# Layer 2's window attention: two windows on the partitions for values and exponentials, their outputs from one 128-row product, the softmax sums beside them

## The chip, the cores and the metric

The kernel runs on one core of one Trainium2 chip, in fp32 throughout. The metric is the device time of one launch in microseconds, the median of several runs. Numbers from "the profile" come from one profiled execution of the kernel, which has a time of its own. The engines are named as in the profile: PE (matrix products; PEld are its weight loads), DVE, ACT, POOL, and SP, which issues most DMAs.

## The reference

Four layers follow one another on 4 images of 192 channels and 64 x 64 pixels: a deformable convolution with channel attention and an MLP (layer 0), a non-local attention (layer 1), an attention over overlapping windows with a gated MLP (layer 2) and a masked, input-dependent 3 x 3 convolution (layer 3). The change is in the window attention of layer 2. Cut to that:

```python
y = _conv1x1(_ln_c(x, n1g, n1b), qkv_w, qkv_b)          # 3*192 channels a pixel
cols = _unfold(y, WS, STRIDE, PAD)                      # windows of 8x8, 6 apart, 3 padding: 11 x 11 of them
win = cols.reshape(B, 3 * HEADS, ch, WS * WS, L).transpose(0, 4, 1, 3, 2)
attn = jnp.einsum('blhic,blhjc->blhij', q, k) + bias    # 6 heads of 32 channels, 64 x 64 pixels
e = jnp.exp(attn - jnp.max(attn, axis=-1, keepdims=True))
s_img = _reverse(jnp.sum(e, axis=-1, keepdims=True), H, W)   # sums, added up over overlapping windows
o = jnp.einsum('blhij,blhjc->blhic', e, v)
o_img = _reverse(o, H, W).reshape(B, HEADS, ch, H, W)        # outputs, added up likewise
out = (o_img / s_img[:, :, None]).reshape(B, C, H, W)
```

## The kernel before, in words

Each image goes through the layers in turn. Layer 0 of the next image is woven into layer 1 of this one and into the end of this one; the window attention, `windows(b, ...)` (L1050), runs alone, between layer 1 and the projection behind it. Inside it the program order is kept by hand (`tc.manual_schedule()`, L1282): every engine takes its instructions in the order in which the loop at L1305 writes them, and only the buffers of a pool are handed out by a planner, which goes by its own costs.

The loop goes over 11 strip rows of windows (`wr`), and in a row over three groups `g` of four windows (the last group has three; a fourth is computed twice and its second copy not used). What a row does, with the lines by which the profile knows it:

- `scores(wr, g)` (L1147): for each of four windows and six heads (3 `e` times 2 `h`) one product of 32 channels, query by key (L1157), into a PSUM tile of three banks, one for each `e`. Before, a window pair lies on the two halves of the partitions (query pixel i of one window on 0 to 63, of the other on 64 to 127), and `h` and key pixel j along the columns. Then DVE adds the position bias (L1164), takes the maximum (L1170) and subtracts it (L1171).
- `exponentials` (L1174): ACT's exponential (L1176), and DVE's two sums of each head (`es`, L1180). They are written one group ahead of use.
- `turned(wr, g, pair)` (L1186): for each of the two window pairs of a group the values: a product of the layer's input with the value weights (L1196), eight of them, so that the two head halves lie on the partitions and the windows side by side in the columns; ACT copies them out (`vs`, L1201). Then three 128 x 128 transposes of the exponentials (L1204) and ACT's copy of them (`et`, L1206). The last pair of a row has a single window.
- `outputs` (L1209), one pair later: for each window, `e` and `h` a product of 64 rows by 32 columns (L1221), which adds the window at its place into the strip `o` in PSUM, and for a pair one product of the sums with shifted identities `pixels` (L1228), which adds the sums into partitions 96 to 101 of the same strip.
- Between them: `norm` of a later row's new pixels (L394 mean, L398 difference, L401 square, L373 variance, L353 and L354 inverse root, L382 its spreading, L413 product), `project_rows` of the next row (L1121 and L1122, copied out by L1125 and L1127), `collect` (L1238, L1239, POOL's L1244), `inverses` (L1260, reciprocal L1264) and `finish` of the row before (L1270, DVE's L1273).

PSUM is fully taken: three banks for scores, two for the strip, one tagged "n" for the norm's products and `inverses`, and two tagged "a", which the values, the transposes, `project_rows` and `finish` share.

## Time and profile before

| | us |
|---|---|
| median of 9 runs | 6755.78 |
| lowest and highest of them | 6728.27 and 6790.15 |
| the profiled execution's own time | 6780.3 |
| its span, first to last instruction | 6778.5 |
| granted PE clock over the span | 0.949 |
| first window stage, 1637.5 to 1903.0 | 265.5, of which PE busy 250.41, DVE 159.86, ACT 119.85, POOL 69.01 |
| the four window stages together | 1074 |

Busy time is the union of an engine's instructions; a run of products is entered with its duration including the time in PE's pipeline, so it overlaps with the next. A span from the start of one block to the start of the next is the better measure of what a block takes, and the prediction uses such spans. In the timeline, "[0.83 <-DVE rs L1264]" after an instruction says that its engine sat idle for 0.83 us before it, and what ended that.

### The profile page before, as it was taken

Reading aid. Unit: us, or ns where it says so; the run is one execution under the profiler, and the core shown is the slowest. Engines: PE = TensorE matmul, PEld = TensorE weight load, DVE = VectorE, ACT = ScalarE, POOL = GpSimd, SP = SyncE. Lnnn points to the kernel's source line nnn. Section 1 sums busy time; section 2 is a strip of 40 time slices with the busy share of each in tenths; the row PEclk is TensorE's granted clock in tenths of the full one; section 3 lists DMA queues with packets and bytes.
Section 4 is the critical chain, followed back from the end, with each engine's and each line's share of the span. In section 5 each row is a group of like instructions: output and inputs, shape, how many; then the busy total and the mean of one; then the engine's idle time right before and its main releaser. Section 6 shows DMA issues by size and latency. Waiting matters only on the chain. (4 is left out here: it accounts for less than half of the span.)

```text
span 6778.5 us, 115795 instructions
## 1 busy us (share of the span) xinstructions
PE 6169.7 (91%) x45392; PEld 4192.4 (62%) x45392; DVE 4696.3 (69%) x6908; ACT 3604.1 (53%) x6136; POOL 2078.0 (31%) x2276
## 2 busy tenths in 40 slices
PE   7687999999989899999998899999998989999986
PEld 4445577877644467787654457878664457776532
DVE  3664258985586849896577848888567767765656
ACT  3664357874445348785445337777444435544332
POOL 2654047761200027773210007675220000002200
PEclk7788989999989999999999999999999999999998
DMA  6786156662010156663110046665100010001000
GB/s 181 254 275 192 46 158 214 212 207 59 10 43 15 42 176 198 220 204 114 33 30 22 19 121 220 210 212 170 38 22 27 17 58 10 15 18 31 4 7 21
DMA packets 330496, 699.37 MB, mean 103 GB/s; under 512 B 60077, under 2 KB 217181, under 8 KB 329182
## 3 DMA queue, kind: packets, MB, share of 16 engines
q0 software_dynamic: 92736, 455.22, 20.6%
q1 hardware_dynamic: 236382, 235.95, 12.2%
q8 instruction: 358, 5.87, 0.4%
q14 instruction: 188, 1.54, 0.1%
q10 hardware_dynamic: 832, 0.79, 0.0%
HBM read 611.25 MB, written 78.87 MB: 102 GB/s over the span
## 5 line engine op out<-in xcount | busy, mean ns | idle before, releaser
L616 POOL DMA_INDIRECT ring<-table,idx x1152 | 1649.2, 1432 | 1139.4 <-DVE row L623 241.9
L963 PE MATMUL s<-ths,ph 96*128 96x256 f32 x4096 | 993.0, 384 | 6.2 <-ACT ths L957 2.4
L963 PEld LDWEIGHTS s<-ths,ph 96*128 96x128 f32 x4096 | 786.2, 193 | 134.4 <-ACT ths L957 5.1
L622 ACT ACTIVATE row<-ring,pos 128x384 f32<-128x384 f32 x1152 | 673.6, 610 | 199.0 <-DVE xo L627 104.1
L1031 PE MATMUL y<-sc,gx 128*97 128x256 f32 x3008 | 728.0, 384 | 32.2 <-ACT yn L1037 27.0
L623 DVE SCALAR_TENSOR_TENSOR row<-ring,fr,row 128x384 f32<-128x384 f32 x1152 | 676.5, 615 | 89.6 <-ACT row L622 60.1
L1031 PEld LDWEIGHTS y<-sc,gx 128*97 128x97 f32 x3008 | 493.6, 166 | 166.7 <-ACT yn L1037 29.4
L626 ACT ACTIVATE xo<-row,pos 128x192 f32<-128x192 f32 x1152 | 488.2, 450 | 163.8 <-remote 71.3
L627 DVE SCALAR_TENSOR_TENSOR xo<-row,fr,xo 128x192 f32<-128x192 f32 x1152 | 449.0, 414 | 125.1 <-ACT xo L626 81.0
L1028 DVE TENSOR_TENSOR sc<-sc,mbs 128x1024 f32<-128x1024 f32 x376 | 454.1, 1220 | 45.1 <-issue 23.4
L965 ACT COPY sc<-s 128x1024 f32<-128x1024 f32 x376 | 377.7, 1005 | 170.8 <-PE s L963 146.2
L970 DVE TENSOR_TENSOR top<-top,sc 128x1024 f32<-128x1024 f32 x282 | 344.9, 1223 | 134.9 <-ACT sc L965 113.9
L634 PE MATMUL h<-ti,xo 128*128 128x192 f32 x2304 | 436.0, 328 | 0.0
L1029 ACT ACTIVATE sc<-sc 128x1024 f32<-128x1024 f32 x376 | 393.9, 1054 | 74.2 <-DVE sc L1028 65.9
L634 PEld LDWEIGHTS h<-ti,xo 128*128 128x128 f32 x2304 | 390.1, 190 | 29.0 <-issue 8.2
L1180 DVE TENSOR_REDUCE es<-ex 128x6 f32<-128x384 f32 x264 | 133.3, 546 | 363.4 <-ACT ex L1176 363.4
L634 PE MATMUL h<-kept,xo 128*128 128x192 f32 x960 | 251.7, 399 | 121.9 <-DVE xo L627 80.6
L634 PEld LDWEIGHTS h<-kept,xo 128*128 128x128 f32 x960 | 182.7, 223 | 212.2 <-DVE xo L627 110.3
L1624 POOL COPY gate<-gate 128x192 f32<-128x192 f32 x12 | 4.2, 351 | 1002.3 <-ACT gate L1617 1002.3
L1377 DVE SCALAR_TENSOR_TENSOR ga<-gate,v,ga 128x1024 f32<-128x1024 f32 x234 | 300.4, 1284 | 6.7
L858 ACT ACTIVATE gl<-h,bias_fc 128x256 f32<-128x256 f32 x384 | 151.2, 474 | 234.0 <-PE h L851 233.5
L1031 PE MATMUL y<-se,gx 128*97 128x256 f32 x1088 | 267.6, 387 | 6.6 <-ACT se L1029 6.0
(391 smaller groups left out, 11239.8 us busy)
## 6 DMA issues: line engine op xcount, KB each, us to landing
ti<-table SPq DMA_DIRECT2D x768, 48.0 KB
ring<-table,idx POOLq DMA_INDIRECT x1152
xnd<-xn SPq DMA_DIRECT2D x4, 3270.0 KB
xi<-in_x_dram SPq DMA_DIRECT2D x32, 384.0 KB
xk<-xd SPq DMA_DIRECT2D x32, 384.0 KB
xd<-xc SPq DMA_DIRECT2D x64, 192.0 KB
table<-tt SPq DMA_DIRECT2D x32, 384.0 KB
xc<-xd SPq DMA_DIRECT2D x60, 192.0 KB
```

What stands on the lines that cost most here:

```text
L616: nc.gpsimd.indirect_dma_start(out=gt.rearrange("p q r c -> p (q r c)"), out_offset=None, in_=corners, in_offset=bass.IndirectOffsetOnAxis ...
L622: nc.scalar.activation(row, gt[:, 0], AF.Copy, scale=pos[:, t, 9 + tap : 10 + tap])
L623: nc.vector.scalar_tensor_tensor(row, gt[:, 1], fr[:, t, 9 + tap : 10 + tap], row, ALU.mult, ALU.add)
L626: nc.scalar.activation(xo[:, j, :], row[:, 0, :], AF.Copy, scale=pos[:, t, tap : tap + 1])
L627: nc.vector.scalar_tensor_tensor(xo[:, j, :], row[:, 1, :], fr[:, t, tap : tap + 1], xo[:, j, :], ALU.mult, ALU.add)
L634: nc.tensor.matmul(acc[m // 2][:, bass.ts(m % 2, C)], lhsT=xo.rearrange("p j c -> p (j c)")[:, bass.ts(m, 128)], rhs=tt, start=t == 0 and ...
L963: nc.tensor.matmul(p[:, t, :], lhsT=ph[:, bass.ts(G * g + t, 128)], rhs=ths[i], start=True, stop=True)
L965: nc.scalar.copy(to, p)
L970: nc.vector.tensor_tensor(tops[i], tops[i], to, ALU.max)
L1028: nc.vector.tensor_tensor(ex, ex, mbs[i].unsqueeze(1).to_broadcast([128, G, QN]), ALU.add)
L1029: nc.scalar.activation(ex, ex, AF.Exp)
L1031: nc.tensor.matmul(py, lhsT=gx[:, G * g + t, :], rhs=ex[:, t, :], start=g == 0 and t == 0, stop=g == NG - 1 and t == G - 1,)
```

## The change

On the partitions of the scores now lie the two head halves `h`, with the windows along the columns. So the transposes yield two windows' key pixels on the 128 partitions, for the three `e` and two `h` in the columns. The values of both windows then come from one product per input half (128 columns of the array, 192 in the moving operand), and the outputs of both windows from one product of 128 rows for each `e` and `h`: the transposed exponentials `et` are written into a tile that is zero elsewhere, the second window six pixels to the right, so that one product of 8 x 14 pixels adds both windows. There are three such tiles an image, cleared once by POOL, and two ACT copies fill one, 64 partitions each. The sums are taken with one DVE instruction a group, spread over the two halves by a product with `side` (1 or 0), and added into the strip by one product for each window, written among the outputs. The bias is loaded directly in the new layout, and the products that keep PE busy at the stage's start (`keep_warm`) read another constant of the same size.

```diff
     for j in range(4):
...
-    pixels = const([128, WS, WS + STRIDE], "pixels")
-    nc.gpsimd.memset(pixels, 0.0)
-    for w in range(2):
-        to = pixels[:, :, STRIDE * w : STRIDE * w + WS]
-        nc.gpsimd.tensor_add(to, to, ident[:, bass.ts(w, WS * WS)].rearrange("p (r c) -> p r c", c=WS))
+    pixels = const([128, WS, WS], "pixels")
+    nc.gpsimd.tensor_add(
+        pixels.rearrange("p r c -> p (r c)"), ident[:, bass.ts(0, WS * WS)], ident[:, bass.ts(1, WS * WS)]
+    )
+    side = const([128, 2], "side")
+    nc.gpsimd.memset(side, 0.0)
+    for h in range(2):
+        nc.gpsimd.memset(side[64 * h : 64 * h + 64, h : h + 1], 1.0)
     eps = const([128, 1], "eps")
...
     headmask = const([P, P], "headmask")
...
-        bias = const([128, 3, 2, WS * WS], "bias")
+        bias = const([128, 3, WS * WS], "bias")
         N1 = 2 * WS - 1
...
             for e in range(HEADS):
...
                     rows = shifted[:, e, :].rearrange("p (r c) -> p r c", c=N1)[:, WS - 1 - ix : 2 * WS - 1 - ix, 0:WS]
-                    in_turn(nc.sync.dma_start(out=bias[WS * ix : WS * ix + WS, e % 3, e // 3, :], in_=rows))
+                    at = 64 * (e // 3) + WS * ix
+                    in_turn(nc.sync.dma_start(out=bias[at : at + WS, e % 3, :], in_=rows))
                 yield
-        in_turn(nc.sync.dma_start(out=bias[64:128], in_=bias[0:64]))
...
     def keep_warm(p, n):
         m, width = p.shape
-        columns = bias.rearrange("p e h j -> p (e h j)")[:, 0:width]
+        columns = spread.rearrange("p j n -> p (j n)")[:, 0:width]
         for _ in range(n):
...
                 sets.append((xs, qs, ks))
+            ets = []
+            for j in range(3):
+                et = s1.tile([128, 3, 2, WS, WS + STRIDE], F32, tag=f"et{j}", name=f"et{j}_{b}")
+                nc.gpsimd.memset(et, 0.0)
+                ets.append(et)
...
             nc.gpsimd.memset(headspread, 0.0)
...
                     for h in range(2):
...
                             rows = slice(32 * e, 32 * e + 32)
-                            at = 128 * (w // 2) + 64 * h
                             nc.tensor.matmul(
-                                p[64 * (w % 2) : 64 * (w % 2) + 64, e, at : at + 64],
+                                p[64 * h : 64 * h + 64, e, 64 * w : 64 * w + 64],
                                 lhsT=qw[rows, h, of, :], rhs=ks[rows, h, :, STRIDE * of : STRIDE * of + WS],
...
                 ex = sb.tile([128, 3, WG, 64], F32, tag="ex", name=f"ex_{b}_{wr}_{g}")
-                half = bias.rearrange("p e h j -> p e (h j)").unsqueeze(2).to_broadcast([128, 3, WG // 2, 128])
                 nc.vector.tensor_tensor(
-                    ex.rearrange("p e (v h) j -> p e v (h j)", h=2),
-                    p[:, :, 0:256].rearrange("p e (v n) -> p e v n", n=128), half, ALU.add,
+                    ex, p[:, :, 0 : 64 * WG].rearrange("p e (w j) -> p e w j", j=64),
+                    bias.unsqueeze(2).to_broadcast([128, 3, WG, 64]), ALU.add,
                 )
...
                 mx = sb.tile([128, 3 * WG], F32, tag="mx", name=f"mx_{b}_{wr}_{g}")
...
             def exponentials(wr, g, ex):
                 nc.scalar.activation(ex, ex, AF.Exp)
-                ex = ex.rearrange("p (e u) j -> p e u j", e=3)
-                sums = sb.tile([128, WG // 2, HEADS], F32, tag="sums", name=f"es_{b}_{wr}_{g}")
-                for pair in range(WG // 2):
-                    nc.vector.tensor_reduce(
-                        sums[:, pair, :].rearrange("p (e h) -> p e h", h=2), ex[:, :, 2 * pair : 2 * pair + 2, :],
-                        AX.X, ALU.add,
-                    )
-                return ex.rearrange("p e u j -> p e (u j)"), sums
+                half = sb.tile([128, WG, 3], F32, tag="half", name=f"eh_{b}_{wr}_{g}")
+                nc.vector.tensor_reduce(
+                    half.rearrange("p w e -> p e w"), ex.rearrange("p (e w) j -> p e w j", e=3), AX.X, ALU.add
+                )
+                sums = sb.tile([128, WG, HEADS], F32, tag="sums", name=f"es_{b}_{wr}_{g}")
+                nc.vector.tensor_tensor(
+                    sums.rearrange("p w (e h) -> p (w e) h", h=2),
+                    half.rearrange("p w e -> p (w e)").unsqueeze(2).to_broadcast([128, 3 * WG, 2]),
+                    side.unsqueeze(1).to_broadcast([128, 3 * WG, 2]), ALU.mult,
+                )
+                return ex.rearrange("p (e w) j -> p e (w j)", e=3), sums
...
                 wins = [w for w in (WG * g + 2 * pair, WG * g + 2 * pair + 1) if w < NWIN]
...
-                pv = ps2.tile([128, 512], F32, tag="a", name=f"v_{b}_{wr}_{g}_{pair}")
-                for i, w in enumerate(wins):
-                    for k in range(2):
-                        for h in range(2):
-                            nc.tensor.matmul(
-                                pv[64 * h : 64 * h + 64, bass.ts(i, P)], lhsT=xw[: P + k, k, w, :],
-                                rhs=qkvT[: P + k, k, 2 * C + P * h : 2 * C + P * h + P], start=k == 0, stop=k == 1,
-                            )
-                v = sb.tile([128, 2, P], F32, tag="v", name=f"vs_{b}_{wr}_{g}_{pair}", bufs=3)
-                nc.scalar.copy(v[:, 0:m, :], pv[:, 0 : m * P].rearrange("p (m c) -> p m c", m=m))
+                rows, both = slice(0, 64 * m), slice(wins[0], wins[0] + m)
+                pv = ps2.tile([128, 512], F32, tag="a", name=f"v_{b}_{wr}_{g}_{pair}")[rows, 0:C]
+                for k in range(2):
+                    nc.tensor.matmul(
+                        pv, lhsT=xw[: P + k, k, both, :].rearrange("p w j -> p (w j)"), rhs=qkvT[: P + k, k, 2 * C :],
+                        start=k == 0, stop=k == 1,
+                    )
+                v = sb.tile([128, C], F32, tag="v", name=f"vs_{b}_{wr}_{g}_{pair}", bufs=3)
+                nc.scalar.copy(v[rows], pv)
                 pt = ps2.tile([128, 512], F32, tag="a", name=f"t_{b}_{wr}_{g}_{pair}")
...
                     nc.tensor.transpose(pt[:, bass.ts(e, 128)], ex[:, e, bass.ts(pair, 128)], ident)
-                et = sb.tile([128, 3, 2, WS, WS], F32, tag="et", name=f"et_{b}_{wr}_{g}_{pair}", bufs=3)
-                nc.scalar.copy(et.rearrange("p e w r c -> p (e w r c)"), pt[:, 0:384])
+                et = ets[(2 * (groups * wr + g) + pair) % 3]
+                for i in range(m):
+                    of = slice(64 * i, 64 * i + 64)
+                    nc.scalar.copy(
+                        et[of, :, :, :, STRIDE * i : STRIDE * i + WS].rearrange("p e h r c -> p (e h r) c"),
+                        pt[of, 0:384].rearrange("p (n c) -> p n c", c=WS),
+                    )
                 return wr, pair, wins, v, et, sums
...
                     pos[wr] = ps.tile([128, 2, WS, W], F32, tag="o", name=f"o_{b}_{wr}")
-                for i, w in enumerate(wins):
-                    c0 = STRIDE * w - PAD
-                    d0, d1 = max(0, -c0), min(WS, W - c0)
-                    first, last = w == 0, w == NWIN - 1
-                    to = pos[wr][:, :, :, c0 + d0 : c0 + d1]
+                first, last = wins[0] == 0, wins[-1] == NWIN - 1
+                rows = slice(0, 64 * len(wins))
+                c0, n = STRIDE * wins[0] - PAD, STRIDE * (len(wins) - 1) + WS
+                d0, d1 = max(0, -c0), min(n, W - c0)
+                for h in range(2):
                     for e in range(3):
-                        for h in range(2):
-                            rows = slice(64 * h, 64 * h + 64)
-                            nc.tensor.matmul(
-                                to[32 * e : 32 * e + 32, h], lhsT=v[rows, i, bass.ts(e, 32)],
-                                rhs=et[rows, e, i, :, d0:d1], start=first, stop=last, skip_group_check=True,
-                            )
-
-                c0, n, m = STRIDE * wins[0] - PAD, STRIDE * (len(wins) - 1) + WS, 64 * len(wins)
-                d0, d1 = max(0, -c0), min(n, W - c0)
-                nc.tensor.matmul(
-                    pos[wr][P : P + HEADS, 0, :, c0 + d0 : c0 + d1], lhsT=sums[:m, pair, :], rhs=pixels[:m, :, d0:d1],
-                    start=wins[0] == 0, stop=wins[-1] == NWIN - 1, skip_group_check=True,
-                )
+                        nc.tensor.matmul(
+                            pos[wr][32 * e : 32 * e + 32, h, :, c0 + d0 : c0 + d1],
+                            lhsT=v[rows, P * h + 32 * e : P * h + 32 * e + 32], rhs=et[rows, e, h, :, d0:d1],
+                            start=first, stop=last, skip_group_check=True,
+                        )
+                    if h < len(wins):
+                        at = STRIDE * wins[h] - PAD
+                        a0, a1 = max(0, -at), min(WS, W - at)
+                        nc.tensor.matmul(
+                            pos[wr][P : P + HEADS, 0, :, at + a0 : at + a1], lhsT=sums[:, 2 * pair + h, :],
+                            rhs=pixels[:, :, a0:a1], start=wins[h] == 0, stop=wins[h] == NWIN - 1, skip_group_check=True,
+                        )
```

## The prediction

> **What bounds the kernel now.** I read the page first, then the stage that the change touches: layer 2's windows, one stretch for each of the 4 images (the first from about 1637 to 1903 us), with nothing of another image beside it. So what the stage gains or loses, the launch gains or loses.

> ```profile
> span 6778.5 us, 115795 instructions
> PE 6169.7 (91%) x45392; PEld 4192.4 (62%) x45392; DVE 4696.3 (69%) x6908; ACT 3604.1 (53%) x6136; POOL 2078.0 (31%) x2276
> ```

> The table of stretches gives PE 250.41 busy us in the first image's 265.5, DVE 159.86, ACT 119.85: PE is the bound on average. The list of PE's waits for 1660 to 1910 us shows where it is not:

> ```profile
> PE pv_l2n L373 <- DVE rs L1264: 6.4, 8, 0.8
> PE t L1204 <- ACT vs L1201: 3.5, 10, 0.4
> ```

> Both recur in every steady strip row (24.9 us: L394 starts at 1762.18 and again at 1787.10). The timeline shows one row; first column the start, second the duration of a run of instructions:

> ```profile
> 1762.27 1.46 PE L394 MATMUL pm_l2n<-xr,mean 96*96 96x384 f32 x4
> 1763.01 1.00 DVE L1180 TENSOR_REDUCE es<-ex 128x6 f32<-128x384 f32 x2
> 1763.65 0.92 PE L1157 MATMUL s<-ks,qw 32*64 32x64 f32 x48
> 1764.49 0.89 PE L1196 MATMUL v<-qkvT,xw 96*64 96x96 f32 x16
> 1765.31 0.55 PE L1204 MATMUL t<-ident,ex 128*128 128x128 f32 x3
> 1765.65 0.30 ACT L1201 COPY vs<-v 128x192 f32<-128x192 f32 x1
> 1766.03 0.89 PE L1121 MATMUL qk<-xs,qkvT 96*96 96x384 f32 x2
> 1768.82 0.89 PE L1196 MATMUL v<-qkvT,xw 96*64 96x96 f32 x16
> ...
> 1773.49 0.91 PE L1157 MATMUL s<-ks,qw 32*64 32x64 f32 x48
> 1774.85 1.01 DVE L1180 TENSOR_REDUCE es<-ex 128x6 f32<-128x384 f32 x2 [7.13 <-ACT ex L1176]
> 1777.87 0.44 PE L1221 MATMUL o<-et,vs 64*32 64x64 f32 x24
> 1778.24 0.36 PE L1228 MATMUL o<-pixels,es 128*6 128x112 f32 x2
> 1778.63 0.75 DVE L1264 RECIPROCAL rs<-sm 128x96 f32<-128x96 f32 x1
> 1779.43 0.54 PE L373 MATMUL pv_l2n<-sq_l2n,mean 96*32 96x96 f32 x16 [0.83 <-DVE rs L1264]
> 1780.41 0.28 ACT L354 ACTIVATE r_l2n<-r_l2n 128x96 f32<-128x96 f32 x1
> 1780.75 0.92 PE L382 MATMUL pb_l2n<-r_l2n,spread 128*96 128x96 f32 x8
> 1784.40 0.55 PE L1196 MATMUL v<-qkvT,xw 96*64 96x96 f32 x8
> 1785.29 0.55 PE L1204 MATMUL t<-ident,ex 128*128 128x128 f32 x3 [0.34 <-ACT vs L1201]
> 1786.42 0.92 PE L1270 MATMUL rb<-rs,headspread 128*96 128x96 f32 x8
> ```

> What to see: PE's blocks follow one another, but at four points another engine is due at the same moment or later. L373 waits for DVE's reciprocal. L382 starts 0.06 us after ACT's L354 ends (1780.69). The first L1121 takes the PSUM buffer that the copy at 1765.65 gives back at 1765.95, 0.08 before. The transposes at 1785.29 wait for the copy of the same pair's values. PE time saved ahead of such a point is lost there.

> **The change on PE.** From the starts of single products in this row: an fp32 product is two instructions, each taking 0.85 ns a column (L1121 and L1122: 384 columns, 0.327 us from one to the next); the first weights of a new array shape cost 0.05; a change of shape costs 0.09 behind the last product (L1228: 0.19 to the next block, of which 0.10 is its own 112 columns).
> - Scores, 3 blocks a row: 0.84 each now. The 48 instructions go to 3 row groups, four in a row to one column half: 0.70 to the last start. After, the halves alternate every three products, so six tiles take 8 each: 0.05 + 8 x 0.056 + 0.09 = 0.59, if they run side by side as L1221's six tiles do (24 instructions of 64 columns, 0.227 to the last start). Bounds 0.59 and 0.84; I take 0.59, -0.25 each.
> - Values of a full pair, 5 a row: 0.82 now. After: 4 instructions of 192 columns at 0.163, 0.65, on the whole array like the transposes behind them, so the 0.09 goes (in layer 0 a 128x192 product is followed by a transpose 0.162 us later), and the transposes' first weights are hidden: their block falls from 0.48 to 0.42. Behind L1122 and L382, also whole-array, another 0.09 goes. Values -0.11 three times, -0.25 twice; transposes -0.06 five times.
> - Outputs and sums of a full pair: 0.37 + 0.29 = 0.66 now (0.58 in the row's first). After, one shape and four column groups. The nearest row is L373: 16 instructions of 96 columns on four column groups, 0.47 to the next block = 0.05 + 4 x 0.083 + 0.09. With 112 columns: 0.05 + 4 x 0.097 + 0.09 = 0.53. -0.13 five times.
> - The single-window pair: values keep one column half, 4 x 0.163 for 4 x 0.083: +0.33. Its outputs have 64 rows, its sums 128 and stand between them: three blocks of 0.05 + 0.10 + 0.09 for one of 0.25: +0.47.

> PE's sum: -0.75 - 0.83 - 0.30 - 0.65 + 0.33 + 0.47 = -1.7 us a row.

> [...]

> **On the other engines.** DVE: per group two sums of 384 elements (0.93 to the next instruction) become one of 768 and a product of 24. The 768 costs what L1170 does (0.95, +0.03 as the next needs it); a product so small is not in the stage. The nearest are layer 3's of one element (0.15) and L1264 (0.75 for 96, a reciprocal); consecutive DVE instructions overlap by 0.09, so 0.06 to 0.2. I take 0.08: 1.06, +0.13 a group. Behind it in DVE's queue stand L398 or the next bias sum, and so both the copy before L1121 and the reciprocal before L373. The bias sum keeps its 768 elements. ACT: `et` is written by two copies of 64 partitions instead of one of 128; time goes with elements a partition, so 0.48 each, 0.38 from start to start. Runs of 8 elements with gaps are in no ACT row; POOL's L1134 writes runs of 6 at 1.2 ns an element and L1109 longer ones at 1.5, so 0.48 is nearest, and up to 0.96 stays in the range. The buffer is given back 0.38 later: 1766.85 where L1121's second product loads at 1767.10; 1783.7 where the last pair's values would want it at 1783.95. Covered, by about 0.25. POOL: three memsets of 672 an image, 0.65 each by the 768 of `headspread` (0.74); POOL has 4.8 us idle there (1.4 in the last image, where the next copy's own 3.1 covers the rest). One bias DMA and the constants: beside layer 0, nothing.

> **What reaches the end, along the row.**
> - L1270 (1761.51) to L1121 (1766.03): PE's blocks end 0.05 later with the single pair's outputs, and DVE's chain (es, L398, then ACT's square and copy) is 0.13 later with little to spare: +0.10.
> - L1121 to the scores at 1773.49: PE alone, except that the transposes at 1769.64 need the buffer of the key copy (ends 1769.47): -0.11 there, then -0.06 and -0.13: -0.30.
> - To L373 (5.94 us): key copy, exponential, es, three DVE passes, reciprocal. PE's saving of 0.9 becomes wait; the chain gains the 0.13: +0.13.
> - To L382: ACT's chain, 0.
> - To L1270: -0.44 up to the last pair's values, then +0.33 and a longer copy before the transposes: -0.08.

> Sum: -0.15 us a row, 8 rows an image, -1.2. The three other rows have no reciprocal wait, but the single pair's outputs end the image: -1 together. Times 4: -9 us. The profiled execution took 6780.3 us (span 6778.5), 24.5 above the median of 6755.78; -9 of it is -0.13%, so 6747 against the median. A measurement of this kernel tells about 0.3% (20 us) from no change.

> **The rivals.** (a) PE sets the row throughout: -1.7 us x 44 = -76 us, 6680. For it: 91% busy and 94% in the stage. Against: L373's wait returns 8 times an image, and three other points have under 0.1 us to spare. Half of it, if the DVE chain is shorter than I make it, is 6718.
> (b) The PSUM buffers change hands, and the time rises. Tag "a" has two. The last pair's transposes now take the buffer of their own values; the other is held by L1270's first product until DVE's L1273 (1786.16, 0.54 long) has read it. If the planner, with the longer copies, hands out that one, the transposes wait until 1786.8 instead of 1785.2: +1.5 us in 40 rows, +60, with the -9: 6807. It decides as soon as the planner expects L1273 before the values' copy; in this trace it is 1.5 us later, which speaks against it.
> (c) The strided copies are dear: past about 0.65 us, two copies no longer fit between one pair's transposes and the next; each 0.1 more costs 0.2 in two or three pairs of a row, some 20 us a launch; 0.96 would give 6800.
> (d) The score tiles do not alternate (0.84 stays): three of the four points hide that anyway; at most +9 us on the forecast, inside it.

> **How the numbers follow.** The forecast has 0.57: it rests on DVE and ACT rows more than on PE's; of it 0.09 ends below -20 us, 0.39 within, 0.09 above. Rival (a), whole or half, 0.20, all faster but 0.01; (b) 0.12 and (c) 0.11, slower but 0.02. So faster 0.28, same 0.42, slower 0.30. The forecast's own range is 6725 to 6775: a small DVE product of 0.2 adds 0.12 at two places of a row, +10, as does (d), and noise of the medians is about as large. The full range reaches past the half of (a), to 6705, and to (c), 6800.

> **What would show it.** Right: PE's busy time in the windows falls by some 60 us over the launch, PE's wait before L373 grows from 0.8 to about 1.7 us, the row stays within 24.6 to 25.0, scores take 0.6 and the output block 0.53. [...]

## The result, and the profile after

The changed kernel takes 6835.47 us in the median of 20 runs (6793.06 to 6858.68), the old one 6763.69 us in the median of 62; the ratio is 1.0096, with a 95% interval of 1.0081 to 1.0111. It is slower by 1%, 72 us, where the forecast was 6747 and the range ended at 6800. The profiled execution took 6799.58 us, near the short end of its runs. The first window stage in it begins 21 us earlier than in the profiled execution of before, so what follows compares stages and rows, not spans.

The page of the changed kernel:

```profile
span 6797.8 us, 106170 instructions
PE 6154.8 (91%) x40376; PEld 4196.9 (62%) x40376; DVE 4719.1 (69%) x6908; ACT 3712.6 (55%) x6356; POOL 2077.7 (31%) x2289
```

PE has 11% fewer products, DVE as many instructions as before, ACT 220 more (the second copy of `et`). The list of PE's waits for one image's steady rows (1660 to 1890 us; total, times, longest):

```profile
PE pv_l2n L376 <- DVE rs L1276: 15.4, 8, 2.0
PE t L1212 <- ACT vs L1209: 3.7, 9, 0.5
```

These are the same two waits as before, L373 now being L376. The first has grown from 0.8 to 2.0 us. The timeline from one group before that wait to the products behind it (start, duration; L1188 is the new product of the sums with `side`):

```profile
1738.40 0.95 DVE L1184 TENSOR_REDUCE eh<-ex 128x12 f32<-128x768 f32 x1 [6.89 <-ACT ex L1182]
1739.45 0.46 DVE L1188 TENSOR_TENSOR es<-eh,side 128x24 f32<-128x24 f32 x1
1739.45 0.43 POOL L1117 COPY xs<-xs 97x272 f32<-97x272 f32 x1
1739.76 0.92 PE L1204 MATMUL v<-qkvT,xw 96*128 96x192 f32 x4
1739.84 0.94 DVE L1170 TENSOR_TENSOR ex<-s,bias 128x768 f32<-128x768 f32 x1
...
1742.68 0.75 DVE L1276 RECIPROCAL rs<-sm 128x96 f32<-128x96 f32 x1
1743.49 0.54 PE L376 MATMUL pv_l2n<-sq_l2n,mean 96*32 96x96 f32 x16 [1.97 <-DVE rs L1276]
...
1745.95 1.54 PE L1204 MATMUL v<-qkvT,xw 96*128 96x192 f32 x4
1746.50 0.18 DVE L1188 TENSOR_TENSOR es<-eh,side 128x24 f32<-128x24 f32 x1
```

Two things are to be seen. DVE's chain to the reciprocal is longer: from the start of the sums (1738.40) to the bias addition (1739.84) it is 1.44 us, where the old timeline has 0.93 (1774.85 to 1775.78); most of the 0.51 between them is L1188, which takes 0.46 us beside the POOL copy L1117 and 0.18 a group later. In the old kernel the same copy (L1109) stood beside the bias addition:

```profile
1775.78 0.95 DVE L1164 TENSOR_TENSOR ex<-s,bias 128x768 f32<-128x768 f32 x1
1775.92 0.41 POOL L1109 COPY xs<-xs 97x272 f32<-97x272 f32 x1
```

And after the wait the same products take longer: L1204's four, 0.92 us at 1739.76, take 1.54 at 1745.95. The table of stretches says why. Each line is a row (two between them, like the second, are left out), from one start of L376 to the next; the columns are the length, the busy times of PE, PEld, DVE, ACT and POOL, the granted PE clock, DMA's share and GB/s:

```profile
1691.47:1716.71 25.24, 22.78 (x348) 15.37 (x348) 15.39 (x21) 13.75 (x29) 6.03 (x17) 1.00 0.05 14
1716.71:1743.49 26.78, 24.35 (x349) 16.79 (x349) 15.40 (x21) 13.75 (x29) 6.04 (x17) 0.94 0.04 12
...
1797.14:1822.39 25.25, 22.78 (x349) 15.38 (x349) 15.38 (x21) 13.76 (x29) 6.03 (x17) 1.00 0.01 2
```

The same view of the old kernel, one row:

```profile
1729.61:1754.52 24.91, 23.74 (x462) 15.70 (x463) 14.75 (x21) 11.33 (x24) 6.61 (x17) 1.00 0.05 14
```

A changed row takes 25.24 us at full clock, 0.33 more than an old one, though PE is busy for 0.96 less. A row at a mean clock of 0.94 takes 1.6 us more again, and of the 28 rows from one such wait to the next in the four images 20 are such rows (26.6 to 27.9 us). Cut into 3.4 us, the stretches show where the clock goes:

```profile
1714.40:1717.80 3.40, 1.45 (x80) 1.06 (x70) 2.22 (x3) 1.34 (x4) 0.00 (x0) 1.00 0.00 0
1717.80:1721.20 3.40, 3.40 (x29) 3.11 (x17) 2.39 (x4) 1.12 (x3) 0.00 (x0) 0.50 0.00 0
...
1792.90:1796.30 3.40, 2.29 (x46) 1.54 (x34) 3.23 (x5) 2.11 (x5) 0.64 (x3) 1.00 0.02 5
1796.30:1799.70 3.40, 2.50 (x75) 2.22 (x76) 1.31 (x3) 1.36 (x3) 0.00 (x0) 1.00 0.00 0
```

The clock falls to half for 3.4 us. The falls of these rows begin at 1717.8, 1745.1, 1772.4, 1823.6 and 1850.9 us, all a whole number of 3.413 us apart: a grid, on which every change of the granted clock in this trace lies, to within 0.01 us. The whole wait before 1716.71 lies in one cell (one step) of the grid, PE is busy there for 1.45 us of 3.40, and the next cell runs at half clock. The wait before 1797.14 is about as long, but the grid cuts it in two, 2.29 and 2.50 us busy, and nothing happens. Of the 32 waits for the reciprocal in the four images (1.7 to 2.0 us each) 23 are followed by half clock; in the old kernel none of its 32 (0.6 to 0.8 us) is. So the theory, called "clock" below: **the change lets PE come earlier to the join at L376 and DVE later; behind the wait of up to 2.0 us the granted clock falls to half in 23 of 32 cases, and that, not the wait, is most of the loss.** For the size of it: in these two executions the four window stages (first to last scores product) take 1063.5 us against 1007.1, so 56 more. Of that 32 rows at 0.33, 11 us, are the chain, and some 45 the clock. The stages' mean clocks agree: 0.94, 0.93, 0.97 and 0.92 over 267.5, 266.9, 260.2 and 268.9 us are 128 us at half clock, for 10 before (1.00, 0.99, 1.00, 0.99), and half of the difference, 59, is the most that this can cost. The runs of the changed kernel go from 6793 us at a mean clock of 0.947, which the profiled one has too, to 6859 at 0.939, so the median run lost more clock than the one shown.

The rival theory, "idle": the idle time and the longer chain are the cost, and the clock only follows where PE has nothing to do anyway.

### The profile page after: what moved, and what is told of

The parts are those of the page before. It is cut to its first block, busy times and chain, and to the rows that moved or that the text cites. A ratio compares the mean times of both kernels' runs of the same rounds, so it can differ in the third digit from the quotient of the medians.

```text
span 6797.8 us, 106170 instructions
## 1 busy us (share of the span) xinstructions
PE 6154.8 (91%) x40376; PEld 4196.9 (62%) x40376; DVE 4719.1 (69%) x6908; ACT 3712.6 (55%) x6356; POOL 2077.7 (31%) x2289
## 5 line engine op out<-in xcount | busy, mean ns | idle before, releaser
L1184 DVE TENSOR_REDUCE eh<-ex 128x12 f32<-128x768 f32 x132 | 125.4, 950 | 360.1 <-ACT ex L1182 360.1
```

## The experiments

The runs of one group shared a chip and the runs of the old kernel on it; the old kernel's median was 6620, 6622 and 6808 us on the three chips, so ratios to that median are compared.

### First group: fill the wait, remove it, or make it

**e1_fill**, the changed kernel:

```diff
                         if wr + 2 < NWIN and g == 1:
+                            for j in range(2 if wr > 0 else 0):
+                                keep_warm(ps2.tile([128, 512], F32, tag="a", name=f"fill_{b}_{wr}_{j}")[:, 0:384], 1)
                             norm(wr + 2, INVERSE)
```

> The changed kernel with two filler products of 384 columns (about 0.65 us each at full clock) put on PE ahead of the variance product L376 in every row after the first, where PE waits 2.0 us for the reciprocal. They compute nothing that is used and lie inside the wait. Theory 'clock' (the idle time before L376 lets the granted clock fall to half for 3.4 us, and that is what the change costs): hardly any time at half clock is left in the four window stages (139 us in the changed kernel's profile, 23 us in the old one's), steady rows go to 25.2 us each, and the kernel to 6755 to 6785 us, near the old kernel. Rival 'idle' (the wait itself and the longer chain on DVE are the cost, the clock only follows): rows stay at 25.2 to 26.9, and the time stays within 10 us of 6835, or goes up if the fillers end later than the reciprocal.

Measured: ratio 1.0016 (0.9998 to 1.0033). What is left of PE's wait is 0.4 us. One row of the table of stretches:

```profile
1619.55:1644.80 25.25, 24.31 (x352) 15.97 (x352) 15.39 (x21) 13.73 (x29) 6.04 (x17) 1.00 0.04 13
```

Work that computes nothing takes back most of the loss: every steady row is 25.25 us at full clock, and the ratio's interval meets neither that of the changed kernel's first runs (1.0081 to 1.0111) nor that of its second (1.0037 to 1.0087, e5 below). The reciprocal comes no earlier; only PE is not idle. What is left agrees with the chain: 0.33 us x 32 rows is 11 us, 0.16%. At other places of the stages some half clock stays (their mean clocks are 0.98, 0.98, 0.99 and 0.97, about 41 us at half clock). The 139 and 23 us of the expectation take in the stages' ends, the 128 and 10 above do not.

**e2_early**, the changed kernel, and **e3_before_early**, the old one, with the same edit, which moves the reciprocal ahead of the scores:

```diff
+                        if wr > 0 and g == 1:
+                            inverses(wr - 1)
                         if nxt[0] < NWIN:
                             sc = scores(*nxt)
...
-                            if wr > 0 and g == 1 and pair == 0:
-                                inverses(wr - 1)
```

> The changed kernel with the sums' four products and their reciprocal moved ahead of the group's scores, so that the reciprocal stands in front of bias, maximum and subtraction in DVE's queue and not behind them. Theory 'clock and DVE order': L376 no longer waits, the idle time and the half clock go, and PE's shorter work shows: rows of 23.3 to 24.5 us, time 6690 to 6740 us. Rival (a): the reciprocal delays the bias addition and the wait goes to the exponentials' users: rows of about 25 us, 6755 to 6790. Rival (b): nothing but the half clock in other places: stays at about 6835.

> Control: the old kernel with the same move of the sums' products and reciprocal. Its wait before the variance product is 0.8 us in each of 8 steady rows of an image and its rows run at full clock, so theory 'clock and DVE order' gives at most 0.8 us x 32 = 26 us: 6735 to 6765 us. If the move is worth as much here as in the changed kernel (70 us or more), it isn't the change's wait that it takes away.

Measured: 0.9932 (0.9907 to 0.9958) for the changed kernel, 0.9956 (0.9934 to 0.9978) for the old one. PE's waits in the changed kernel's steady rows (1608 to 1726 us), and one row of it:

```profile
PE t L1212 <- ACT vs L1209: 2.0, 5, 0.4
PE pb_l2n L385 <- ACT r_l2n L357: 1.2, 5, 0.2
```

```profile
1631.71:1655.20 23.49, 22.80 (x361) 15.42 (x352) 15.23 (x22) 13.85 (x30) 6.00 (x17) 1.00 0.05 15
```

With the reciprocal ahead in DVE's queue L376 no longer waits, and rows fall to 23.5 us, as theory "clock and DVE order" had it; its ratio lies inside the expected band (6690 to 6740 of 6764 us is 0.989 to 0.996). The control gains 1.0 us a row, to 23.9, where 0.8 was expected:

```profile
1612.06:1635.94 23.88, 23.54 (x471) 15.76 (x465) 14.69 (x22) 11.32 (x25) 6.59 (x17) 1.00 0.05 14
```

The move takes 1.75 us off a changed row at full clock and 1.0 off an old one: what the change had saved on PE had become wait. Where neither kernel waits for the reciprocal, the change is worth 0.4 us a row.

**e4_before_delay**, the old kernel, nothing of the change in it:

```diff
                             if wr > 0 and g == 1 and pair == 0:
+                                for j in range(3):
+                                    idle = sb.tile([128, 6], F32, tag="idle", name=f"idle_{b}_{wr}_{j}")
+                                    nc.vector.tensor_reduce(idle, bias.rearrange("p e h j -> p (e h) j"), AX.X, ALU.max)
                                 inverses(wr - 1)
```

> The old kernel with three more DVE reductions over the bias tile (about 0.44 us each, 1.3 us in all; results unused) ahead of the reciprocal in each row after the first: nothing of the change, but a wait before the variance product of 2.0 us and over, as the changed kernel has it. Theory 'clock': the granted clock falls to half for 3.4 us after most of these waits (100 us or more at half clock in the four window stages, 23 us in the old kernel's profile), rows of 26.2 plus 1.7 us, and a time of 6764 + 1.3 x 36 + some 50 = about 6860 us. Rival 'idle': rows of 26.2 us at full clock, 6764 + 47 = about 6811 us.

Measured: 1.0222 (1.0192 to 1.0252), 154 us; the rival's 47 us are far off, and theory "clock" was too low with its 96. PE's wait (1632 to 1750 us) and a row:

```profile
PE pv_l2n L373 <- DVE rs L1264: 11.0, 5, 2.2
```

```profile
1661.96:1690.74 28.78, 26.24 (x463) 17.70 (x463) 16.21 (x24) 11.30 (x24) 6.59 (x17) 0.90 0.05 13
```

DVE is busy for 1.46 us more, the rows are 3.9 to 4.3 us longer, at a clock of 0.87 to 0.90. The old kernel alone, with a wait like that of the changed one, loses its clock in every row, for some 6 to 8 us each (twice 0.10 of 28.8, twice 0.13 of 29.2).

### Second group: the threshold, and the short DVE product

**e5_after**, the changed kernel once more. 

> The changed kernel as it is, beside the next three and the old kernel on their chip, so that they can be compared. Theory 'clock': ratio to the old kernel 1.008 to 1.012, rows of 25.2 us at full clock and 26.7 to 26.9 in the others, 130 us or so at half clock in the four window stages.

 Measured: 1.0062 (1.0037 to 1.0087), lower than expected, with an interval that overlaps the first; rows of 25.2 and 26.7 to 26.8 us; the four stages 1059.2 us at mean clocks of 0.91, 0.96, 0.97 and 0.95.

**e7_before_delay1**, the old kernel with one of e4's three reductions.

> The old kernel with one DVE reduction (0.44 us, unused) ahead of the reciprocal in each row after the first: a wait before the variance product of 1.2 to 1.3 us, between the old kernel's 0.8 and the changed one's 2.0. Theory 'clock': where the half clock begins is not known. If 1.3 us is still short enough, the rows are 25.3 us at full clock and the ratio 1.002 to 1.004; if it is too long, rows of 26 to 28 us and a ratio over 1.008. Rival 'idle': 25.3 us and 1.002 to 1.003 in any case.

Measured: 1.0101 (1.0075 to 1.0126). The wait (1598 to 1733 us) and two rows:

```profile
PE pv_l2n L373 <- DVE rs L1264: 7.7, 6, 1.3
```

```profile
1625.11:1653.43 28.32, 26.69 (x463) 17.98 (x463) 15.29 (x22) 11.30 (x24) 6.59 (x17) 0.88 0.04 12
1653.43:1678.79 25.36, 23.74 (x462) 15.70 (x462) 15.21 (x22) 11.30 (x24) 6.59 (x17) 1.00 0.05 14
```

The rows before and behind these are like them: 26.81 at a clock of 0.94, 25.37 at 1.00. A wait of 1.3 us is already too long in 15 of 28 cases in the four images (three of the five rows from 1598.30 to 1732.40 us are at 0.94, 0.88 and 0.88); the old kernel's 0.83 is in none of 28, and e4's 2.0 to 2.2 us in all of 32. At full clock the added reduction costs what it takes, 25.36 for 24.91; half a microsecond of DVE work then costs the launch 1%, most of it through the clock (0.45 us x 32 is 0.2%). That is the branch of the expectation in which 1.3 us is too long.

**e6_fill_side**, e1 with the product of `half` and `side` written in another form:

```diff
-                nc.vector.tensor_tensor(
-                    sums.rearrange("p w (e h) -> p (w e) h", h=2),
-                    half.rearrange("p w e -> p (w e)").unsqueeze(2).to_broadcast([128, 3 * WG, 2]),
-                    side.unsqueeze(1).to_broadcast([128, 3 * WG, 2]), ALU.mult,
-                )
+                for h in range(2):
+                    nc.vector.tensor_scalar_mul(
+                        sums.rearrange("p w (e h) -> p (w e) h", h=2)[:, :, h],
+                        half.rearrange("p w e -> p (w e)"), side[:, h : h + 1],
+                    )
```

> The changed kernel with the two filler products ahead of L376 (rows 25.2 us at full clock, ratio 1.0016 without the next edit), and its product of sums and side written as two products with a scalar for each partition, so that DVE reads one tensor from SBUF and not two. Theory 'blocked read' (the product L1188 takes 0.46 us instead of 0.18 in the group whose product lies beside a POOL copy, and this is in the chain that sets the row): the two take 0.2 to 0.3 together there, the rows fall to 25.0 to 25.1 us, 8 to 15 us in all, ratio 0.9995 to 1.0005. Rival 'any short instruction is that dear' (the 0.46 is a wait for the reduction before it): each of the two takes as much or their sum is 0.46 or over; rows 25.2 us or longer.

Measured: 1.0040 (1.0022 to 1.0058), rows of 25.5 us: slower than e1. The timeline of the two products away from the POOL copy, and beside it:

```profile
1629.68 0.37 DVE L1189 TENSOR_SCALAR es<-eh,side 128x12 f32<-128x12 f32 x2
...
1641.63 0.41 POOL L1117 COPY xs<-xs 97x272 f32<-97x272 f32 x1
1641.65 0.55 DVE L1189 TENSOR_SCALAR es<-eh,side 128x12 f32<-128x12 f32 x2
```

The expectation missed, and the signs named for its rival are met: a sum over 0.46 and rows over 25.2. The rival's reason is not, since a single L1188 takes 0.18 away from the copy. Two instructions cost more than one anywhere (0.37 for 0.18), and beside the copy they are slowed too, though less (by 0.18, not by 0.28). So reading one tensor in place of two is no way out, and whether two reads are the cause stayed open here; e9 below moves the copy.

**e8_early_warm**, e2 with fillers at three more waits of a stage (`filler(name, n)` writes n products like those of e1):

```diff
+                        if wr == 1 and g == 0:
+                            filler(f"{b}_{wr}", 2)
                         if wr + 2 < NWIN and g == 0:
...
                 collect(NWIN - 1)
+                filler(f"{b}_last", 2)
                 inverses(NWIN - 1)
+                filler(f"{b}_end", 1)
```

> The changed kernel with the reciprocal moved ahead of the scores (ratio 0.9932), and filler products at the three other places of a stage where PE waits over 0.9 us and the clock halves after it: two before the mean of the fourth strip in row 1, two before the last row's sums, one before its inverses are spread. Theory 'clock': the half clock in the four window stages falls from 64 us to 30 or less, 15 us off the time, ratio 0.990 to 0.992. Rival: the half clock stands for other waits (the start of the stage) and the ratio stays 0.993.

Measured: 0.9929 (0.9907 to 0.9952). From the first to the last scores product the half clock in the four stages went from 61 us to none, and the stages from 981.0 to 957.4 us in the profiled executions, as the theory had it. But the ratio is the rival's 0.993 and not the 0.990 to 0.992 expected, and it moved by less than the intervals can tell. The profiled execution of e2 was the longest of its runs (6603.26 for a median of 6575.85) and had the lowest mean clock of them (0.955; the median is 0.9585, as of e8's runs), so its 61 us may have been more than usual; that isn't settled.

### Third group: the copy moved, and the change by itself

**e9_fill_pool**, e1 with POOL's copy put off:

```diff
                         if g == 2 and wr + 2 < NWIN:
+                            idle = s1.tile([128, 512], F32, tag="idle", name=f"idle_{b}_{wr}")
+                            nc.gpsimd.memset(idle, 0.0)
+                            nc.gpsimd.memset(idle, 0.0)
                             shared(wr + 2, 0)
```

> The changed kernel with the two filler products ahead of L376 (rows 25.2 us at full clock), and two memsets of an unused tile (512 elements a partition, about 0.5 us each) in POOL's queue ahead of the copy L1117 of xs, so that the copy starts about 1 us later and no longer beside the product L1188. Theory 'POOL copy' (it is the copy that makes the product 0.45 us instead of 0.18): the product takes 0.18 again, unless the memset has the same effect, and the rows fall to 24.95 us, provided that the copy does not lengthen the DVE passes that it now lies beside; ratio about 1.000. Rival 'phase' (the product is slow in that group whatever POOL does, for example since PE's weight load from the strip's sums starts at the same moment): 0.45 us and 25.2 us as before.

Measured: 0.9993 (0.9964 to 1.0022). The timeline at the same place:

```profile
1683.16 0.52 POOL L1356 MEMSET idle<- 128x512 f32 x1
1683.16 0.18 DVE L1188 TENSOR_TENSOR es<-eh,side 128x24 f32<-128x24 f32 x1
...
1684.21 0.41 POOL L1117 COPY xs<-xs 97x272 f32<-97x272 f32 x1
```

With a memset beside it the product takes 0.18 us again, and a row takes 25.0 at full clock (1682 to 1707 us): the copy L1117 slows it, a memset does not, and the rival "phase" falls. The rows show this; the ratios of e1 and e9 overlap. The chain's 0.33 us a row is thus for the most part, 0.25, this meeting of two instructions. Not every POOL copy does it: in the changed kernel's profile all 32 products beside L1117 took 0.43 to 0.46 us, but the eight that lay beside the smaller copies L1143 or L1144 alone took 0.18, as here:

```profile
1869.25 0.33 POOL L1143 COPY xw<-xs 97x160 f32<-97x160 f32 x1
1869.44 0.18 DVE L1188 TENSOR_TENSOR es<-eh,side 128x24 f32<-128x24 f32 x1
```

**e10_before_early_warm** and **e11_early_warm**: the edits of e8 in the old kernel and, once more, in the changed one.

> Control for the next: the old kernel with the reciprocal ahead of the scores and the same filler products at the three other places. Its rows are 23.9 us with the early reciprocal and its half clock in the window stages is 24 us, so there is at most 12 us to win on the ratio of 0.9956: 0.993 to 0.996.

> The changed kernel with the early reciprocal and the fillers once more, beside its control on one chip. With no wait for the reciprocal and no half clock in the window stages on either side, what is left is the change's own work: rows of 23.5 us against 23.9, 0.4 x 32 = 13 us, and the single-window ends of the stages; theory 'clock' expects 10 to 25 us less than the control. Rival: the changed kernel's half clock is in its nature and the two are within 5 us.

Measured: 0.9937 (0.9909 to 0.9964) for the old kernel, 0.9921 (0.9896 to 0.9947) for the changed one; medians 6769.29 and 6759.77 us. The window stage of the second image in each, the old kernel's first:

```profile
3237.80:3481.70 243.90, 237.43 (x4789) 159.99 (x4788) 150.84 (x214) 114.49 (x243) 67.59 (x183) 1.00 0.09 25
```

```profile
3206.90:3446.00 239.10, 228.98 (x3615) 155.87 (x3614) 156.01 (x214) 140.83 (x295) 63.64 (x183) 1.00 0.09 24
```

Both stages run at full clock, and the changed one is 4.8 us shorter. Summed over the four images the stages take 977.3 and 957.4 us; 13 of these 20 us are the steady rows, 23.9 against 23.5, and some 3 are a fall of the clock that was left in the old kernel's first stage (mean clock 0.99). The medians differ by 9.5 us, just under the 10 to 25 expected; the intervals overlap, so the runs do not settle the order of the two. Both are faster than the old kernel, by 0.6% and 0.8%.

## Why the prediction was wrong

**The failed step: PE's idle time was priced at nothing.** "PE's saving of 0.9 becomes wait" was right in kind, and the wait it led to, 1.7 us, is not far from the 1.97 measured (its own terms, 0.83 and 0.9 and the chain's 0.13, add up to 1.86). But the working stopped there, as if PE stood still and went on as before. e1 (the wait filled, the clock back) and e4 and e7 (the wait made in the old kernel, the clock lost) show from both sides what such a wait brings: in the changed kernel half clock for 3.4 us behind 20 of the 32, for 6.8 behind three. e1 gives back 0.5 to 0.8% (1.0062 and 1.0096 less 1.0016), 31 to 54 us, and the rest is about the chain's 11. No rival had it, so the range could not reach it; the nearest price in the forecast's own row was L373's wait of 0.83 us, and the clock fell behind none of its 32.

**The term of the small DVE product was mis-sized.** It was taken as 0.08, with 0.06 to 0.2 as bounds and 1.06 us from the sums to the next instruction. Measured: 1.07 to 1.09 in the groups away from POOL's copy, and 1.44 in the group that leads to the reciprocal. Hence 0.51 in place of 0.13 in that chain, rows of 25.24 in place of 24.6 to 25.0, and 11 us. The price of the meeting with POOL's copy was left out, though the copy (L1109) stood at that place in the old timeline.

**PE saved half of what was forecast, which hardly mattered.** By the starts of blocks in e3 and e2, which differ by the change alone:

| a row | forecast | measured |
|---|---|---|
| scores, 3 blocks | -0.75 | -0.35 (0.73 each: six tiles do alternate, but the first weights take 0.11, and behind the last start comes 0.145 as before) |
| values and transposes, with the blocks ahead of them and the finish | -0.80 | -0.18 (the values' first weights, 128 columns, take 0.11 in every pair) |
| outputs and sums | -0.18 | -0.19 |

So -0.7 for -1.7. Of it 0.4 reaches the row of e2; most of the rest became waits, 0.23 us before L385 above all. Ahead of L376 it was about 0.6 for 0.9, while the chain grew by 0.51 for 0.13; the forecast wait came out nearly right since the two errors offset each other. Had PE saved all of it, the wait would only have been longer.

**The rivals.** (a) PE sets the row: not in this kernel, but nearly so in e2, where it is worth 0.4 us a row and not 1.7. (b) The buffers: the last pair's transposes still wait for the copy of their values, 0.5 us at most, and not for L1285. (c) Dear copies: a copy of `et` takes 0.48 us, as taken; from start to start it is 0.5, not 0.38. (d) The score tiles do alternate. An output block takes 0.51 us by its starts, for 0.53 forecast.

## What to carry to other kernels

Before taking work off PE ahead of a point where it waits for another engine, look at how long it will then sit there: here the granted clock stayed up behind all 32 waits of the old kernel (0.6 to 0.8 us) and fell to half behind 23 of the changed one's 32 (1.7 to 2.0 us), which the table of stretches cut to 3.4 us shows. If the wait grows past about a microsecond (an estimate from these runs: 0.83 us never cost any clock, 1.3 us did in half of the cases), move the awaited instruction forward in the other engine's queue (here a reciprocal ahead of three passes, 1.75 us a row), or else fill the wait with products that nobody reads. And for a short DVE instruction look at what POOL does at that moment, not only at its size: here 24 elements took 0.18 us alone and 0.43 to 0.46 beside one POOL copy.

## What the runs showed of the hardware

A DVE product of 24 elements took 0.18 us alone, 0.43 to 0.46 beside a POOL copy of 272 elements, and 0.18 beside a POOL memset or POOL copies of 160 and 16 elements, if POOL's spans are right, which are rough in this profile. DVE's scalar form in e6, with one tensor from SBUF, was slowed as well, from 0.37 to 0.55 us for two, so a second tensor does not explain it alone. Why one copy slows the product and the smaller ones do not, no run here tells.
